# A transformer layer on one Trainium2 core: the product with W_o as seven quarter products, norms whose inverse roots are iterated on VectorE and applied by ScalarE

## The chip, the cores and the metric

The kernel runs on one core of a Trainium2 chip. That core has five engines which run their own instruction streams and wait for one another by semaphores: TensorE (PE; its weight loads are listed apart as PEld), VectorE (DVE), ScalarE (ACT), GpSimd (POOL) and SyncE (SP), which here issues nearly all DMAs. The metric is the device time of one execution in microseconds (us). The kernel before takes 535.52 us, the median of three runs (535.15 to 535.86).

## The reference

The input x is 4 x 2048 tokens of 256 features, in float32, taken as 8192 tokens in a row. The layer has two halves, each with a residual and a layer norm.

```
Q, K, V = x W_q^T, x W_k^T, x W_v^T
S = (Q K^T) * mask          # in chunks of 32 tokens, mask[i,j] = decay^(i-j) for i >= j
O = S V
attn = sigmoid(x W_g^T) * O @ W_o^T + x
h = layernorm(x + attn)     # so 2x + (gate * O) W_o^T
ffn = (silu(h Wg^T) * (h Wu^T)) Wd^T    # integer weights / 127, hidden size 768
out = layernorm(h + ffn)
layernorm(z) = (z - mean) / sqrt(var + 1e-5)
```

## The kernel before

The tokens are cut into 16 blocks of 512 (`TB`); a block is four groups of 128 tokens (`NG`). x is loaded twice, once with tokens and once with features on the partitions (`load_xn`, `load_xT`).

**Attention of a block.** W_q and W_k are folded into one matrix at the start (`make_m`), so there are four products with 256x256 matrices: y, v, the gate, and W_o. From block 2 on, the first three are made by `seven`: a block Strassen scheme (Winograd's form) in which the matrix and the block's operand are cut into quarters, seven products of sums of quarters replace eight, and VectorE, ScalarE and GpSimd add the results. `weight_sums` makes the sums of the matrix once, `token_sums` those of a block on GpSimd (four operations, L353 to L356). `seven` issues four products into four PSUM banks, lets ScalarE copy three of them (L406), VectorE form u (L408) and GpSimd p57 (L410); the function that it returns (`others`) adds the other three products onto banks 1, 5 and 7, and writes the four quarters of the result: one on ScalarE (L416), two on VectorE (L417, L418), one on GpSimd (L419). `token_major` (v) uses products of 128x128 by 128 columns, `feature_major` (y, gate) of 256 columns. `attn_scores` (PE L514, VectorE L524) and `attn_values` (PE L535, VectorE L542) make gate times O, `goT`.

**W_o and the first norm.** `attn_out` multiplies goT by W_o in `project_back` (16 matmuls of 256 columns, L561, tile pa), adds 2x on VectorE (L582), and calls `layer_norm`: statistics on VectorE (`moments`, L295 and L296), the root on ScalarE (`root`, L304), the reciprocal and a rescaling on VectorE (L315, L317), and four scalings of 128x256 on VectorE (L319).

**Moving h.** The FFN needs h with features on the partitions. `move_h` transposes h in squares of 32 on VectorE (four instructions, L616) and puts the squares in place by 16 DMAs on SP's queue (L622); `split_h` rounds hT to a high part on ScalarE (L639) and a float16 rest on GpSimd (L640). The buffers of `move_h` exist once, those of `split_h` twice.

**FFN.** `ffn_up` makes one chunk of 128 hidden features at a time (six chunks): eight matmuls of 512 columns (L656), the sigmoid on ScalarE (L664), two products on VectorE (L666, L668), then the high part on ScalarE (L675) and the rest on GpSimd (L676). `ffn_down` is `project_back` again (48 matmuls L561, tile fdn), with the residual on VectorE (L683). `finish` norms and stores (L691).

**Order.** Loop turn b makes the FFN of block b, the attention from the scores on of block n = b + 2, and the products v, y and gate of block m = b + 3. The code interleaves these by hand, and a scheduler orders each engine's stream from it: earlier lines first among what it takes to be ready by its own model of times; `tc.keep_in_program_order` (`in_turn`) pins an instruction behind all that its engine was given before. PSUM has eight banks of one tag, handed out as they come free. In every turn the PE order is: chunk 0, chunk 1, scores of n, chunk 2, first v products of m, chunk 3, rest of v, values of n, first y products, chunk 4, rest of y, chunk 5, first gate products, pa of n, rest of gate, fdn of b. The last turn (b = 13) has no block m.

**Head and tail.** The head does the attention of blocks 0 and 1 and the y, v and gate of block 2. One half of a weight matrix is looked up for its largest entry at the end of each of the first six turns (`look_up`, L261), and `count_wide` turns that into a count that a branch at the end reads (for weights that the two-part split could not hold exactly, a second path follows; it isn't taken on these inputs). After the loop come the FFNs of blocks 14 and 15. The last `ffn_down` goes group by group (PE L853, residual L861), and norms block 14 and the four groups of block 15 between (root L304, reciprocal L806 or L876, shift on GpSimd L815, scaling on ScalarE L824, the last on VectorE L877), each group with its own store (L838).

Of the kernel before, what the change touches and what calls it, by code (L numbers as in the profile page):

```python
# [70 lines left out]
def kernel(  # L71
# [184 lines left out]
    top = const.tile([P, 6], F32, tag="top", name="top")  # L256

    def look_up(i):
        w = (fg, fu, fd)[i // 2][0].bitcast(F32)
        half = w.shape[1] // 2  # L260
        reduced = nc.vector.tensor_reduce(  # L261
            top[:, i : i + 1],
            w[:, i % 2 * half : (i % 2 + 1) * half, :].rearrange("p k n -> p (k n)"),
            mybir.AxisListType.X,
            ALU.max,
            apply_absolute_value=True,
        )
        tc.keep_in_program_order(reduced)
# [21 lines left out]
    def moments(r, name, groups=range(NG), order=free):  # L290

        mv = small.tile([P, NG, 2], F32, tag="mv", name=f"mv_{name}")
# [17 lines left out]
    def layer_norm(dst, r, name, on_r=1.0, on_dst=1.0):  # L310
# [7 lines left out]
        for g in range(NG):  # L318
            nc.vector.tensor_scalar(  # L319
                dst[:, g, :],  # L320
# [4 lines left out]
                ALU.mult,  # L325
            )
# [21 lines left out]
    def token_sums(t, name):  # L348

        out = sums.tile([P, 4, HB], F32, tag="sums", name=f"{name}_sums")  # L350
        t1, t3, t2, t4 = (out[:, i, :] for i in range(4))
        b11, b12, b21, b22 = (t[:, k, n * HB : (n + 1) * HB] for k in range(2) for n in range(2))
        nc.gpsimd.tensor_tensor(t1, b12, b11, ALU.subtract)  # L353
# [5 lines left out]
    def feature_major(a, b):  # L359


        def product(i, pb, first):
            nc.tensor.matmul(  # L363
                pb,
                lhsT=a[i - 1],
                rhs=b[i - 1],
                start=first,
                stop=True,
                skip_group_check=True,
            )  # L370

        return product

    def token_major(a, b):


        def product(i, pb, first):
            for g in range(HB // P):
                nc.tensor.matmul(  # L379
                    pb[:, g * P : (g + 1) * P],  # L380
                    lhsT=b[i - 1][:, g * P : (g + 1) * P],
                    rhs=a[i - 1],
                    start=first and g == 0,
                    stop=True,
                    skip_group_check=True,
                )

        return product

    def seven(name, product, quarter, func=AF.Copy):  # L390
# [9 lines left out]
        banks = {i: bank(f"p{i}_{name}")[:, :HB] for i in (1, 5, 7, 6)}  # L400
# [11 lines left out]
        def others():  # L412
            for i, onto in ((2, 1), (3, 5), (4, 7)):
                product(i, banks[onto], False)
# [579 lines left out]
```

## Time and profile before

| what | value |
|---|---|
| median of 3 runs | 535.52 us |
| profiled execution, its own time | 535.63 us |
| its span | 533.9 us |
| mean granted TensorE clock | 0.995 |
| PE / PEld / DVE / ACT / POOL busy | 522.8 / 421.0 / 391.2 / 310.8 / 268.4 us |
| one loop turn in the middle (371.2 to 403.2 us) | 32.0 us |
| in that turn PE / DVE / ACT / POOL busy | 32.00 / 23.64 / 19.19 / 17.14 us |

The span is what the trace covers; the profiled execution's own time is 1.7 us longer. Busy time is the time in which an engine had an instruction under way; PE's matmuls overlap and their ends are modelled, so that a PE which is always busy can still run slower than it could.

### The profile page before, as it was taken

The numbers are of one execution on the slowest core, as the hardware profiler recorded it, in microseconds if no ns is written. First come the engines' busy times: TensorE is split into PE (matmuls) and PEld (weight loads), VectorE is DVE, ScalarE is ACT, GpSimd is POOL, SyncE is SP. The second block draws the span as 40 slices with busy tenths as digits, with TensorE's granted clock in tenths as the row PEclk, the third lists the DMA queues.
The fourth block names the chain that finished last, engine by engine and source line by source line (L and its number), as shares of the span: only waits on it lengthen the run. The fifth ranks groups of instructions, "written<-read, shape, count | busy, mean of one in ns | idle before, by whom it ended". The sixth has DMA issues, their size and how long they took to land.

```text
span 533.9 us, 9939 instructions
## 1 busy us (share of the span) xinstructions
PE 522.8 (98%) x3486; PEld 421.0 (79%) x3486; DVE 391.2 (73%) x1026; ACT 310.8 (58%) x561; POOL 268.4 (50%) x305
## 2 busy tenths in 40 slices
PE   8999999999999999999999999999999999999992
PEld 5688887888878788887888878788887888868792
DVE  4468659587695867859587695867859587698883
ACT  2284556555564754656555664764657566566754
POOL 5132672735636365572735636374572736433651
PEclk9999999999999999999999999999999999999997
DMA  7531312214130231412214130231412113020102
GB/s 253 181 120 39 80 40 69 52 41 119 42 101 18 52 108 41 114 46 63 58 39 120 41 105 15 54 107 40 112 49 78 42 43 78 1 65 16 40 2 82
DMA packets 43126, 36.87 MB, mean 69 GB/s; under 512 B 4673, under 2 KB 38977, under 8 KB 43073
## 3 DMA queue, kind: packets, MB, share of 16 engines
q1 hardware_dynamic: 41952, 35.15, 23.3%
q10 hardware_dynamic: 1088, 1.05, 0.6%
q8 instruction: 29, 0.48, 0.4%
q14 instruction: 25, 0.20, 0.1%
q0 software_dynamic: 32, 0.00, 0.0%
HBM read 20.45 MB, written 8.39 MB: 54 GB/s over the span
## 4 chain that ended last, share of the span: by engine, by line
PE 95%; DVE 2%; ACT 1%; issue 0%; DVEq 0%; POOL 0%
PE fg L656 16%; PE fdn L561 16%; PE fu L656 15%; PE pa L561 10%; PE p_v L379 8%; PE p_y L363 8%; PE p_g L363 8%; PE po L535 5%; PE ps L514 3%; PE pg L459 1%; PE py L475 1%; PE pv L494 1%; PE pi L177 1%; DVE u L668 1%; DVE s L666 1%
## 5 line engine op out<-in xcount | busy, mean ns | idle before, releaser
L676 POOL TENSOR_TENSOR u_lo<-u,u_hi 128x512 f16<-128x512 f32 (+1 forms) x102 | 123.7, 1214 | 144.3 <-ACT u_hi L675 143.8
L666 DVE SCALAR_TENSOR_TENSOR s<-fg,s 128x512 f32<-128x512 f32 (+1 forms) x102 | 66.4, 651 | 48.1 <-ACT s L664 47.6
L664 ACT ACTIVATE s<-fg 128x512 f32<-128x512 f32 (+1 forms) x102 | 58.2, 571 | 66.6 <-PE fg L656 65.9
L675 ACT CAST u_hi<-u 128x512 fp32r<-128x512 f32 (+1 forms) x102 | 60.4, 592 | 31.5 <-DVE u L668 30.7
L656 PE MATMUL fg<-hT_hi,fg_hi 128*128 128x512 f32 (+1 forms) x204 | 74.0, 443 | 0.0
L668 DVE TENSOR_TENSOR u<-fu,s 128x512 f32<-128x512 f32 (+1 forms) x102 | 66.1, 650 | 5.0 <-POOL u_lo L676 1.0
L656 PE MATMUL fu<-hT_hi,fu_hi 128*128 128x512 f32 (+1 forms) x204 | 61.6, 382 | 0.0
L656 PE MATMUL fg<-hT_lo,fg_lo 128*128 128x512 f16 (+1 forms) x204 | 58.9, 370 | 0.0
L656 PE MATMUL fu<-hT_lo,fu_lo 128*128 128x512 f16 (+1 forms) x204 | 58.1, 366 | 0.0
L561 PE MATMUL pa<-wo,goT 128*128 128x256 f32 x256 | 58.0, 379 | 0.0
L561 PE MATMUL fdn<-fd_hi,u_hi 128*128 128x256 f32 x360 | 55.4, 296 | 0.0
L561 PEld LDWEIGHTS pa<-wo,goT 128*128 128x128 f32 x256 | 48.6, 190 | 6.7
L640 POOL TENSOR_TENSOR hT_lo<-hT,hT_hi 128x512 f16<-128x512 f32 x28 | 35.4, 1286 | 28.5 <-ACT hT_hi L639 28.5
L561 PEld LDWEIGHTS fdn<-fd_hi,u_hi 128*128 128x128 f32 x360 | 46.8, 189 | 1.1
L561 PE MATMUL fdn<-fd_lo,u_lo 128*128 128x256 f16 x360 | 44.7, 274 | 0.0
L656 PEld LDWEIGHTS fu<-hT_hi,fu_hi 128*128 128x128 f32 x204 | 37.5, 188 | 7.7
L656 PEld LDWEIGHTS fg<-hT_hi,fg_hi 128*128 128x128 f32 x204 | 35.7, 189 | 8.5
L304 ACT ACT_TABLE_LOAD x30 | 38.5, 1283 | 0.5
L656 PEld LDWEIGHTS <-fu_lo 128*128 128x128 f16 x204 | 20.0, 98 | 21.5 <-DVE sT L524 1.2
L561 PEld LDWEIGHTS <-u_lo 128*128 128x128 f16 x360 | 32.7, 98 | 5.1 <-POOL u_lo L676 0.3
L582 DVE SCALAR_TENSOR_TENSOR h<-x,pa 128x512 f32<-128x512 f32 x32 | 22.0, 688 | 17.5 <-PE pa L561 16.9
L535 PE MATMUL po<-sT,v 128*128 128x128 f32 x256 | 31.2, 275 | 0.0
(150 smaller groups left out, 983.7 us busy)
## 6 DMA issues: line engine op xcount, KB each, us to landing
x<-in_x_dram SPq DMA_DIRECT2D x16, 512.0 KB, 3.4
xT<-in_xT_dram SPq DMA_DIRECT2D x15, 512.0 KB, 4.4
out_dram<-r SPq DMA_DIRECT2D x15, 512.0 KB, 5.1
hT<-sq SPq DMA_DIRECT2D x224, 32.0 KB, 1.9
fg_int<-in_ffn_gT_dram SPq DMA_DIRECT2D x3, 256.0 KB, 8.1
fu_int<-in_ffn_uT_dram SPq DMA_DIRECT2D x3, 256.0 KB, 6.5
fd_int<-in_ffn_dT_dram SPq DMA_DIRECT2D x3, 256.0 KB, 6.0
xT<-in_xT_dram SPq DMA_DIRECT2D x2, 256.0 KB, 3.8
```

The source lines that it names most:

```text
L304: nc.scalar.activation(std[:, span], mv[:, span, 1], AF.Sqrt, bias=eps, scale=1 / on_r**2)
L363: nc.tensor.matmul(pb, lhsT=a[i - 1], rhs=b[i - 1], start=first, stop=True, skip_group_check=True,)
L379: nc.tensor.matmul(pb[:, g * P : (g + 1) * P], lhsT=b[i - 1][:, g * P : (g + 1) * P], rhs=a[i - 1], start=first and g == 0, stop=True, ski ...
L535: nc.tensor.matmul(po[:, cols], lhsT=v[:, g, dc * P : (dc + 1) * P], rhs=sT[:, cols], start=True, stop=True,)
L561: nc.tensor.matmul(pb[:, j * D : (j + 1) * D], lhsT=part[:, g * P : (g + 1) * P], rhs=w, start=(i == 0), stop=(i == len(terms) - 1),)
L640: nc.gpsimd.tensor_tensor(in_order[1], whole, in_order[0].bitcast(F32), ALU.subtract)
L656: nc.tensor.matmul(pb, lhsT=w[kind][:, dc, hc * P : (hc + 1) * P], rhs=hT[kind][:, dc, cols], start=(kind == kinds[0] and dc == 0), stop=( ...
L664: nc.scalar.activation(s, pg, AF.Sigmoid, scale=SCALE / H_UP)
L666: nc.vector.scalar_tensor_tensor(s, pg, U_UP / H_UP**2, s, ALU.mult, ALU.mult)
L668: nc.vector.tensor_tensor(u, pu, s, ALU.mult)
L675: nc.scalar.copy(hi, u)
L676: nc.gpsimd.tensor_tensor(lo, u, hi.bitcast(F32), ALU.subtract)
```

## The change

1. **W_o.** For blocks 2 to 14 (the 13 turns that have a block m), `attn_out` is replaced by `split_out`: goT is summed in quarters on GpSimd (`token_sums`, with a buffer of its own), `seven` makes the product with `token_major` (28 matmuls of 128 columns), the residual 2x + product is added to the first quarter from PSUM and to the other three by VectorE afterwards, c22 is added on VectorE and not on GpSimd, and the moments are taken. `weight_sums` of W_o is made in the head. In `seven` the first four products go in the order 1, 6, 5, 7, and the matmuls of `others` are pinned in program order.
2. **Norms in the loop.** `split_out` and `ffn_down` only take the moments. One turn later `scale_and_shift` makes, for h of that turn and the FFN's r together, 1/sqrt by a bit trick and two iteration steps on VectorE (15 small instructions on 128x4 or 128x8), and `normalize` applies scale and shift by four ScalarE activations each. So `move_h` comes later in the turn (after the first v products of m), `split_h` at the end of the turn, and the store of r_b in turn b + 1. Chunks 4 and 5 of `ffn_up` are issued together, and the rest of y after both.
3. **Look-ups.** Nine reductions, one for each loaded integer piece, in the head; `count_wide` in turn 0.
4. **Tail.** The scalings of block 14 are spread over ScalarE (groups 0, 1) and GpSimd (2, 3), those of block 15 over ScalarE (0, 1) and VectorE (2, 3); block 14 is stored last, from ScalarE's queue.

```diff
-    def look_up(i):
-        w = (fg, fu, fd)[i // 2][0].bitcast(F32)
...
+    def look_up():
+        for i, piece in enumerate(piece for pieces in ffn_int for piece in pieces):
+            nc.vector.tensor_reduce(
+                top[:, i : i + 1], piece.rearrange("p k n -> p (k n)"),
...
+    def scale_and_shift(parts, name):
...
+        for c, (mv, on_r, on_dst) in zip(cols, parts):
+            nc.vector.tensor_scalar(v[:, c], mv[:, :, 1], 1 / on_dst**2,
+                EPS * (on_r / on_dst) ** 2, ALU.mult, ALU.add)
+        nc.vector.tensor_scalar(
+            guess, v.bitcast(I32), -0.5, float(0x5F3759DF), ALU.mult, ALU.add)
+        nc.vector.tensor_copy(y.bitcast(I32), guess)
+        times(t, y, y)
+        times(t, t, v)
+        nc.vector.tensor_scalar(q, t, 0.375, -1.25, ALU.mult, ALU.add)
+        times(q, q, t)
+        nc.vector.scalar_tensor_tensor(y, q, 1.875, y, ALU.add, ALU.mult)
+        times(t, y, y)
+        times(t, t, v)
+        nc.vector.tensor_scalar(t, t, -0.5, 1.5, ALU.mult, ALU.add)
+        times(y, y, t)
+        for c, (mv, _, _) in zip(cols, parts):
+            nc.vector.scalar_tensor_tensor(
+                shift[:, c], mv[:, :, 0], -1.0, y[:, c], ALU.mult, ALU.mult)
+        return [(y[:, c], shift[:, c]) for c in cols]
+
+    def normalize(r, scale, shift):
+        for g in range(NG):
+            nc.scalar.activation(r[:, g, :], r[:, g, :], AF.Identity,
+                bias=shift[:, g : g + 1], scale=scale[:, g : g + 1])
...
+    def split_out(b, goT_sums):
...
+        others = seven(f"o_{b}", token_major(w_sums["o"], goT_sums), quarter,
+            first=lambda _, product: residual(0, 0, product), last=nc.vector)
+
+        def rest():
+            others()
+            residual(1, 0, quarter(1, 0))
+            gs = slice(NG // 2, NG)
+            nc.vector.scalar_tensor_tensor(
+                flat(r, gs), flat(xn, gs), 2.0, flat(r, gs), ALU.mult, ALU.add)
+            return moments(r, f"a{b}")
...
         sT = attn_scores(n, yT)
+        if b:
+            mvs = (late[0][1], 1.0, H_UP), (late[1][1], H_UP, 1.0)
+            of_h, of_out = scale_and_shift(mvs, f"{b}")
         if m + 1 < NB:
             xTs[m + 1] = load_xT(m + 1)
-        moving = move_h(b + 1, hs[b + 1])
+        if not more:
+            normalize(late[0][0], *of_h)
+            moving = move_h(b + 1, hs[b + 1])
         ffn_up(b, hT, uT, range(2, 3))
         if more:
             v_next, v_rest = split_v(m, x_sums)
+            if b:
+                normalize(late[0][0], *of_h)
+            moving = move_h(b + 1, hs[b + 1])
...
         goT = attn_values(n, sT, v, sg)
+        if b:
+            normalize(late[1][0], *of_out)
+            store(b - 1, late[1][0])
+        else:
+            n_wide = count_wide()
         if more:
+            go_sums = token_sums(goT, f"go_{n}")
             y_next, y_rest = split_y(m, x_sums)
-        ffn_up(b, hT, uT, range(4, 5))
+        ffn_up(b, hT, uT, range(4, KH))
         if more:
             y_rest()
-            hTs[b + 1] = split_h(b + 1, moving)
-        ffn_up(b, hT, uT, range(5, KH))
-        if more:
-            sg_next, g_rest = split_gate(m, x_sums)
-        hs[n] = attn_out(n, goT, 1 if n == NB - 1 else H_UP)
-        if more:
+            sg_next, g_rest = split_gate(m, x_sums)
+            hs[n], out_rest = split_out(n, go_sums)
             g_rest()
+            mv_h = out_rest()
+            hTs[b + 1] = split_h(b + 1, moving)
+            if m + 1 < NB:
+                x_sums = token_sums(xTs[m + 1], f"x_{m + 1}", in_turn)
+            r, mv = ffn_down(b, uT, hs.pop(b))
+            late = [(hs[n], mv_h), (r, mv)]
+        else:
+            hs[n] = attn_out(n, goT, 1)
+            r, mv = ffn_down(b, uT, hs.pop(b))
+            hTs[b + 1] = split_h(b + 1, moving)
+            ((scale, shift),) = scale_and_shift([(mv, H_UP, 1.0)], f"{b + 1}")
+            normalize(r, scale, shift)
+            store(b, r)
...
+        if g == 1:
+            inverse(std_before, slice(0, NG), H_UP)
+            mv, std = of_group[0]
+            inverse(std, slice(0, 1))
+            shift = shift_of(nc.gpsimd, 0, mv, std)
+            in_turn(nc.gpsimd.tensor_tensor(shift_before, minus_mean, std_before, ALU.mult))
+            by_scalar(r, 0, std, shift)
+            store_group(0)
+            for g_before in (2, 3):
+                by_vector(nc.gpsimd, r_before, g_before, mv_before, std_before)
+            by_scalar(r_before, 0, std_before, shift_before[:, 0:1])
+        if g == 2:
+            mv, std = of_group[1]
+            inverse(std, slice(1, 2))
+            by_scalar(r, 1, std, shift_of(nc.vector, 1, mv, std))
+            store_group(1)
+    by_scalar(r_before, 1, std_before, shift_before[:, 1:2])
+    for g in (2, 3):
+        mv, std = of_group[g]
+        inverse(std, slice(g, g + 1))
+        by_vector(nc.vector, r, g, mv, std)
+        store_group(g)
+    in_turn(nc.scalar.dma_start(
+        out[(last - 1) * TB : last * TB, :].rearrange("(g p) d -> p g d", p=P), r_before))
```

## The prediction

> **What bounds the kernel now.** I read the page's busy shares first, then busy time by stage, then the chain, then the tail's instructions in order of time.
>
> ```profile
> span 533.9 us, 9939 instructions
> ...
> PE 522.8 (98%) x3486; PEld 421.0 (79%) x3486; DVE 391.2 (73%) x1026; ACT 310.8 (58%) x561; POOL 268.4 (50%) x305
> ...
> PE 95%; DVE 2%; ACT 1%; issue 0%; DVEq 0%; POOL 0%
> ```
>
> PE is 98% of the span and 95% of the chain. The stretches (length, then PE, PEld, DVE, ACT, POOL busy) show where the rest is: a middle turn has no PE gap, the tail's 15.4 us hold 5.83 us of PE.
>
> ```profile
> 371.20:403.20 32.00, 32.00 (x218) 26.08 (x217) 23.64 (x62) 19.19 (x34) 17.14 (x18) 1.00 0.24 67
> ...
> 490.10:518.50 28.40, 28.36 (x202) 22.68 (x201) 24.22 (x62) 17.43 (x38) 13.89 (x15) 1.00 0.06 20
> 518.50:533.90 15.40, 5.83 (x51) 5.26 (x50) 6.67 (x25) 7.75 (x17) 4.26 (x11) 0.82 0.22 71
> ```
>
> So in the loop time falls only by less PE work, and rises as soon as anything holds PE; in the tail the norm's chain counts. The chain in order of time (start, us, what) prices the two ways to make a 256x256 product: the old W_o and the seven quarters of v.
>
> ```profile
> 377.96 1.78 PE p_v L379 x16
> ...
> 381.52 1.34 PE p_v L379 x12
> ...
> 393.00 3.45 PE pa L561 x16
> ```
>
> The tail, in order of time:
>
> ```profile
> 522.53 0.42 DVE L861 SCALAR_TENSOR_TENSOR r<-fdn,h 128x256 f32<-128x256 f32 x1
> ...
> 523.03 2.07 ACT L824 ACTIVATE r<-r,shift_f,rstd_f 128x256 f32<-128x256 f32 x4 [0.82 <-POOL shift_f L815]
> ...
> 525.01 0.47 ACT L304 ACTIVATE rstd_f<-mv_f,eps 128x1 f32<-128x1 f32 x2
> 525.13 0.38 SPq L691 DMA_DIRECT2D out_dram<-r  x1
> 525.32 0.16 DVE L806 RECIPROCAL rstd_f<-rstd_f 128x1 f32<-128x1 f32 x1 [1.69 <-ACT rstd_f L304]
> ...
> 526.50 3.23 SPq L838 DMA_DIRECT2D out_dram<-r  x4
> ...
> 528.58 0.41 DVE L877 TENSOR_SCALAR r<-r,mv_f,rstd_f 128x256 f32<-128x256 f32 x1
> ```
>
> PE's last matmul ends at 524.3, but DVE stands idle 1.69 us behind ScalarE's four scalings of block 14, so the last residual starts only at 526.93 and the last scaling ends at 528.99.
>
> **What the Trainium skill says.** "ScalarE: Activation LUTs", What ACT_TABLE_LOAD costs: a load takes about 1283 ns, and an activation about 186 ns + 0.833 ns per element, 93 ns more for each pointer operand, with 93 ns of overlap back to back. The trace agrees: 1283 ns on every load; four pointer-fed scalings of 256 in 2.07 us, 0.49 apart. Same page, Table sets: copy and identity are in every set. The trace agrees in that L824 follows the root with no load, and sigmoids follow copies with none. "GPSIMD Engine Reference", Engine selection: two-input work costs about twice VectorE's. Here 0.73 us (L353) against 0.42 (L408). "Perfetto Trace Analysis", Identifying the Most-Contended Engine: matmul busy time says little on how near PE is to its limit. Here I therefore use issue distances (3.45 us for 16), not mean durations (379 ns).
>
> **The change part by part.** Turn times are counted from the end of the previous fdn.
>
> *W_o, 13 turns.* Old 3.45 us. New 1.78 + 1.34 = 3.12 us, since it is v's form. Saved 0.33 x 13 = **4.3 us** of PE, all on the path. What it adds elsewhere per turn: GpSimd four sums and one p57, 5 x 0.73 = 3.65 us, so 17.1 becomes 20.8 of 31.7; ScalarE three copies of 0.37; VectorE u, three quarters, two residual quarters and one half, 6 x 0.34 + 0.6 = 2.6 us in place of two residuals (1.2). Cover: goT is done at about 14.5, its sums by about 17.5, and split_out's first product comes at 21.4: 3.9 us of slack. The copies of banks 1, 5, 7 have the 1.29 us of the gate's rest before the product on bank 1, and more for 7, which waits for two others first.
>
> *Norms.* ScalarE loses four table loads (5.1 us) and two roots (0.6) per turn and gets eight activations of 0.49 (3.9): no more work. VectorE loses eight scalings (8 x 0.34) and two pairs of small steps (0.7), and gets 15 small dependent ones; L315 and L317 start 0.2 apart, so 3.0 us. With W_o's, VectorE's sum is +1.0 us per turn, 23.6 to about 24.7 of 31.7. Queued behind these 15 are the chunks' s and u, which free PSUM banks. Before, the same stretch (0 to 9.6) held block b's scalings and part of the transposes. By my count u of chunk 2 ends at 9.8 (9.6 before), then the four transposes (1.5) fill a wait of 1.2 us for ScalarE, and goT ends at 14.6 (14.1 before). The first y products at 13.1 to 14.8 need v's last quarters off their banks (12.3 and 13.2): about 0.5 us of room. I take a loss of **0**; without that cover it costs what VectorE is late, once per turn.
>
> *h moved later.* scale_and_shift ends at about 6 to 8, ScalarE's normalize at 8.5 to 10.5, the last transpose at 9 to 11. The 16 DMAs leave 0.63 us apart behind one another on SP (10.1 us), with the load of xT (0.59) and the store (0.46) in the same queue; the last lands 1.9 us after issue, at 22 to 24.4. split_h is pinned behind the gate's last sigmoid, about 26.6: high part to 27.8, rest to 29.8, and chunk 0 wants them at 31.3 and 32.2. Hidden, with 2.4 us to spare (10 before). Then x's sums follow to 0.9 of the next turn, wanted at 6.4. The last turn is short (467.24 to 490.08, 22.84 us): scale ends 6 to 8, normalize 8.2 to 10.2, transposes 8.7 to 10.7, the last DMA lands 20.7 to 22.7, high part 21.9 to 23.9, rest 23.9 to 25.9, wanted at 22.8 and 23.9: a stall of 0 to 2, I take **1.0**.
>
> *Stores.* r_b leaves a turn later; two r buffers cover it. The x load on SP waits for the residual either way.
>
> *Look-ups.* Six of 0.945 us leave the loop. Nine of 128x512 come into the head, about 0.65 each by the ratio of elements, 5.9 us. The pieces land by 22.2, VectorE idles 3.9 us before the scores at 25.9, and the rest delays a yT copy by about 0.9 us, which the values' 1.78 us on PE hide. No row shows where the order puts them: if one stands ahead of m_sb or yT and waits for its piece, 1 to 4 us. I take **0**. W_o's sums (5 x 0.45 on GpSimd) fall into its wait of 5.3 us. count_wide's matmul (0.12) only moves.
>
> *Tail.* VectorE loses count and n_wide (0.3 us in front of the first residual). The residuals then follow PE: g1 about 521.5, g2 523.1 after three small steps, g3 524.6 after PE's end at 524.2. Statistics to 525.65, root of g3 on ScalarE 525.67 to 525.97, while VectorE scales r2 (525.85 to 526.26); reciprocal and r3 end at 526.9. Against 528.99 that is 2.1 us. ScalarE's scaling of block 14's group 1 ends at 526.5, then its store leaves: the same store took 3.2 us at 525.13, so it lands at about 530, and r3's (issue 527.25, 2.7) at 530.0, where the old last one landed near 532.4. GpSimd's scaling of 128x256 has no row; from 0.53 for 128x128 I take 0.95, twice to 525.6, and even at 1.4 it ends by 526.5. A store of 5.1 us, as in the loop, would leave 0.7 of the gain. I take **2.0**.
>
> Sum: -4.3 - 2.0 + 1.0 = -5.3. Span 533.9 to 528.6; with the 1.7 us around it 530.3 against 535.63 profiled, so **530.2** against the median 535.52.
>
> **The rivals.** *Given back in part:* a store of 5.1 us, a head stall, or 0.1 to 0.3 us of bank waits per turn. For it: the room of 0.5 us is small, and the waits before show
>
> ```profile
> PEld ps L514 <- DVE s L666: 4.8, 13, 0.4
> ```
>
> a bank freed by VectorE just in time in each turn. Against: PE never stood. With 0.2 x 13 = 2.6 lost: 532.8. *Slower:* VectorE becomes the bound in the first half of a turn. Place: the 15 steps, or transposes that wait for ScalarE's scalings, stand ahead of s and u or of v's quarters, and PE waits at the first y product. Price: each us that VectorE is late beyond 0.5 costs PE one us per turn; the gain of 5.3 is gone at 0.41 per turn, and at 0.8 it is 10.4 lost, 540.6. For it: VectorE has some 12.6 us of work between 2 and 15. Against: it idles over 4 us in the second half, and much of what went was in this half. *hT late in every turn:* needs 2.4 us more than my times; then it is slower in the same way. *No change in PE:* products of 128 columns that run slower than v's; against it stands the same form's 3.12 us in each turn.
>
> **How the numbers follow.** A run tells 0.2% (1.1 us) from no change. As worked out, 528 to 532: 0.60. Given back in part, 532 to 534.4: 0.17. Gains and losses even: 0.05. Slower, by VectorE or hT: 0.18. Faster 0.77, same 0.05, slower 0.18. The range 528 to 536 leaves out most of the slower case and little below, where only a tail at its floor (PE's end plus the 2.06 us from the last residual to the last scaling) would lie. The likeliest case alone has 528 to 532.
>
> **What would show it.** A middle turn of 31.67 us with PE busy throughout; no pa row in it and the o products 1.78 + 1.34; ScalarE with few table loads; DVE near 24.7 per turn; PE's end to DVE's end 2.7 us in the tail, not 4.7. Wrong would be: PE gaps before p_y or ps released by VectorE, or before chunk 0 released by hT; a wait of PE in the head; a last store landing after 531.

## The result and the profile after

The changed kernel takes 575.77 us (median of 4 runs, 573.65 to 576.99), the kernel before in the same comparison 535.69 us (535.15 to 536.49): a ratio of 1.074, 95% interval 1.070 to 1.078. It is slower by 40 us, where 5 us less had been forecast. The profiled execution took 574.92 us, its span is 573.1 us.

The page of the changed kernel, span, busy shares and chain by engine:

```profile
span 573.1 us, 10619 instructions
...
PE 533.4 (93%) x3642; PEld 428.0 (75%) x3642; DVE 455.1 (79%) x1143; ACT 287.9 (50%) x624; POOL 328.4 (57%) x372
...
PE 43%; DVE 42%; issue 6%; ACT 3%; DMA 3%; SPq 2%; POOL 1%; DVEq 0%; ACTq 0%
```

PE was 95% of the chain; now it has 43% and VectorE 42%. VectorE's busy time rose by 64 us although the forecast gave it 1 us more per turn; an instruction that is held counts as busy. By stage (length, then PE, PEld, DVE, ACT, POOL busy, granted clock, DMA share, GB/s), a middle turn, turn 13, and blocks 14 and 15 up to PE's last product:

```profile
361.71:395.47 33.76, 32.19 (x230) 26.32 (x229) 28.38 (x71) 17.53 (x39) 21.58 (x24) 1.00 0.21 63
...
498.39:526.50 28.11, 24.29 (x162) 17.34 (x160) 25.75 (x73) 12.94 (x24) 7.65 (x6) 1.00 0.13 39
526.50:564.57 38.07, 36.60 (x248) 28.41 (x248) 28.79 (x78) 22.67 (x50) 20.05 (x23) 0.96 0.04 15
```

A turn grew from 32.0 to 33.76 us, though PE still has only some 32 us of work in it. Summed over the span, 39.2 us were lost:

| stretch | before | after | lost |
|---|---|---|---|
| start to the end of turn 0 | 83.08 | 89.94 | +6.86 |
| turns 1 to 12 | 384.00 | 408.45 | +24.45 |
| turn 13 | 22.84 | 28.11 | +5.27 |
| blocks 14, 15 to the last product | 34.41 | 38.07 | +3.66 |
| last product to the end of the span | 9.55 | 8.52 | -1.03 |

Of the 24.45 us of turns 1 to 12, 3.3 are not the same in every turn: ten turns took 33.75 to 33.78 us, and two took 35.4, at a mean granted clock of 0.95. In blocks 14 and 15, PE's gaps are 1.5 us of the 3.66, and its busy time is 2.2 us longer, at a granted clock of 0.96 in place of 1.00.

The waits of the changed kernel (who, for what; us in all, number, longest in us):

```profile
ACT h L375 <- DVE shift L368: 29.5, 13, 2.5
...
PEld p_v L437 <- ACT p_v L466: 19.2, 12, 1.6
...
PE py L539 <- DVE m_sb L198: 5.4, 1, 5.4
```

So the reader is to see three things: PE waits once per turn for a copy of v's product on ScalarE, ScalarE waits for VectorE's small steps (`shift`), and once, in the head, PE waits 5.4 us for m_sb.

**Where VectorE's time is.** The trace of one turn of the changed kernel, VectorE and GpSimd merged in order of time (start, duration, engine, line, out<-in; the bracket is idle time ahead and what ended it; the duration of a row "x2" runs from the start of the first to the end of the second):

```profile
390.56 2.98 POOL L735 TENSOR_TENSOR hT_lo<-hT,hT_hi 128x512 f16<-128x512 f32 x2
390.90 1.49 DVE L662 SCALAR_TENSOR_TENSOR h<-x,h 128x256 f32<-128x256 f32 x1
392.31 1.77 DVE L678 SCALAR_TENSOR_TENSOR h<-x,h 128x512 f32<-128x512 f32 x1
...
401.30 1.26 POOL L771 TENSOR_TENSOR u_lo<-u,u_hi 128x512 f16<-128x512 f32 x1 [5.00 <-ACT u_hi L770]
401.55 1.03 DVE L342 TENSOR_TENSOR q<-q,t 128x8 f32<-128x8 f32 x1
...
403.91 1.27 POOL L771 TENSOR_TENSOR u_lo<-u,u_hi 128x512 f16<-128x512 f32 x1 [1.35 <-ACT u_hi L770]
403.98 1.22 DVE L362 SCALAR_TENSOR_TENSOR y<-q,y 128x8 f32<-128x8 f32 x1
405.24 0.17 DVE L342 TENSOR_TENSOR t<-y 128x8 f32<-128x8 f32 x1
```

Two of the small steps, eight numbers per partition, take 1.03 and 1.22 us; the step right after, of the same size, takes 0.17, and so do the later ones with two tiles as input, beside which GpSimd runs nothing. The long ones end when GpSimd's instruction ends: 401.55 + 1.03 = 402.58 against 401.30 + 1.26 = 402.56, and 405.20 against 405.18. The residuals fit less closely: the two hT_lo, 1.55 and 1.47 us, end at 392.10 and 393.53, and the residuals 0.29 and 0.55 us later (392.39 and 394.08), a little less than the 0.42 and 0.68 that they take for their own work.

**What stands behind.** ScalarE and PE of the same turn, in order of time:

```profile
404.23 0.36 ACT L466 COPY p_v<-p_v 128x256 f32<-128x256 f32 x1
406.84 0.60 ACT L375 ACTIVATE h<-h,shift,y 128x256 f32<-128x256 f32 x1 [2.25 <-DVE shift L368]
407.35 0.35 ACT L466 COPY p_v<-p_v 128x256 f32<-128x256 f32 x1
407.60 0.62 ACT L770 CAST u_hi<-u 128x512 fp32r<-128x512 f32 x1
407.75 0.71 PE L437 MATMUL p_v<-v_sums,xT 128*128 128x128 f32 x4 [1.40 <-ACT p_v L466]
408.12 0.37 ACT L466 COPY p_v<-p_v 128x256 f32<-128x256 f32 x1
408.63 0.57 PE L437 MATMUL p_v<-v_sums,x_sums 128*128 128x128 f32 x3 [0.17 <-ACT p_v L466]
```

The second and third copy of v's product do not need the norm, but they stand behind h's scaling, which waits for the steps. The third also stands behind u_hi of chunk 2, whose u VectorE makes after the steps and ends only at 407.56. PE's v products wait for those copies. Set beside a turn of e12_best (below), PE starts every group of products up to here at the same time to within 0.04 us, and everything after the twelve later products of v comes 2.1 us later: they take 3.4 us in place of 1.34. So the loss of a turn arises at this one place.

**The hypothesis (H) that this reading gives.** A VectorE instruction with both inputs in SBUF (the on-chip memory of the tiles; PSUM holds PE's results) waits for the GpSimd instruction under way; what is late by that goes through ScalarE's queue to PE. The rivals: the order of ScalarE's queue is the cause (R1); VectorE simply has too many instructions (R2); W_o's sevens come too late in the turn, wherever the norms are (R3). The Trainium skill has H's first half, "SBUF — State Buffer", Who interferes with whom: "A DVE instruction with two SBUF inputs contends with a GpSimd instruction that reads SBUF", and it calls what they share an exclusive lock, where issue order decides who blocks. The ends of the small steps above agree with it to 0.02 us.

### The profile page after: what moved, and what is told of

The parts are those of the page before. It is cut to its first block, busy times and chain, and to the rows that moved or that the text cites. A ratio compares the mean times of both kernels' runs of the same rounds, so it can differ in the third digit from the quotient of the medians.

```text
span 573.1 us, 10619 instructions
## 1 busy us (share of the span) xinstructions
PE 533.4 (93%) x3642; PEld 428.0 (75%) x3642; DVE 455.1 (79%) x1143; ACT 287.9 (50%) x624; POOL 328.4 (57%) x372
## 4 chain that ended last, share of the span: by engine, by line
PE 43%; DVE 42%; issue 6%; ACT 3%; DMA 3%; SPq 2%; POOL 1%; DVEq 0%; ACTq 0%
PE p_y L419 7%; PE p_g L419 7%; PE fg L751 6%; PE fu L751 6%; PE po L599 5%; DVE s L761 5%; DVE h L662 4%; PE p_o L437 4%; DVE h L678 4%; DVE u L763 4%; DVE st_f L297 4%; DVE y L362 3%; DVE r L780 3%; PE p_v L437 3%; DVE st_a L297 2%
## 5 line engine op out<-in xcount | busy, mean ns | idle before, releaser
L735 POOL TENSOR_TENSOR hT_lo<-hT,hT_hi 128x512 f16<-128x512 f32 x28 | 41.2, 1493 | 10.3 <-ACT hT_hi L734 9.8
L375 ACT ACTIVATE h<-h,shift,y 128x256 f32<-128x256 f32 x52 | 28.3, 597 | 29.5 <-DVE shift L368 29.5
L599 PE MATMUL po<-sT,v 128*128 128x128 f32 x256 | 34.2, 291 | 0.0
L599 PEld LDWEIGHTS po<-sT,v 128*128 128x128 f32 x256 | 33.0, 208 | 0.8 <-issue 0.5
L437 PE MATMUL p_v<-v_sums,x_sums 128*128 128x128 f32 x224 | 30.9, 282 | 2.1 <-ACT p_v L466 2.1
L711 DVE STREAM_TRANSPOSE sq<-h 128x256 f32<-128x256 f32 x56 | 24.4, 440 | 10.6 <-ACT h L375 9.3
```

Of the source, the lines that this page charges most:

```text
L437: nc.tensor.matmul(pb[:, g * P : (g + 1) * P], lhsT=b[i - 1][:, g * P : (g + 1) * P], rhs=a[i - 1], start=first and g == 0, stop=True, ski ...
L599: nc.tensor.matmul(po[:, cols], lhsT=v[:, g, dc * P : (dc + 1) * P], rhs=sT[:, cols], start=True, stop=True,)
L735: nc.gpsimd.tensor_tensor(in_order[1], whole, in_order[0].bitcast(F32), ALU.subtract)
```

## The experiments

Each kernel is the changed one with the edit shown, except where another base is named. The kernel before took 535.35 to 536.02 us beside them. e1 to e8 and e10 are one run each. "Turn" is a turn from the middle of the loop, read from the trace (32.0 us before, 33.76 after).

### e1_lookups: part 3 undone

```diff
-    look_up()                      # nine reductions, in the head
+            if b < 6:
+                look_up(b)         # one 128x768 at the end of a turn, pinned
+        if b == 8:
+            n_wide = count_wide()
```

> Part 3 of the change undone: the six look-ups of 128x768 stand at the ends of turns 0 to 5 again, the count in turn 8. As a side effect ScalarE's order in the loop becomes: all three copies of v's first products, then the four scalings of h (in the changed kernel a scaling of h stands between the first and the second copy). Theory H (the head's loss is VectorE waiting for an integer piece in front of m_sb): the head's wait of 5.43 us in front of y is gone and the slow y products after it, so that turn 0 ends near 83.1 us and not at 89.9. Rival (the head's loss comes from W_o's sums on GpSimd or from the clock): turn 0 still ends above 88. In the loop, theory A (see e2_pin) expects turns of 31.7 to 32.4 us, so about 545 to 553 in all; its rival 33 us or more, so about 565.

Measured: 566.59 us. Turn 0 ends at 83.02 (89.94 after, 83.08 before): the head's loss is wholly that of the look-ups. The head of the changed kernel shows how, in order of time:

```profile
15.43 0.69 DVE L261 TENSOR_REDUCE top<-fg_int 128x1 f32<-128x512 int32 x1 [3.36 <-DMA fg_int<-in_ffn_gT_dram]
...
22.18 0.69 DVE L198 COPY m_sb<-pm 128x512 f32<-128x512 f32 x1
...
22.93 5.22 PE L539 MATMUL py<-xT,m_sb 128*128 128x512 f32 x8 [5.43 <-DVE m_sb L198]
```

Five look-ups were put ahead of m_sb, 0.69 us each, and the first waited 3.36 us for its piece; m_sb came at 22.18 instead of 16.15. Then the y products themselves took 5.22 us instead of 3.60. "TensorE: Matmul & The Clock Gate", What's actually happening, says that PE's clock is halved after an idle window of about 3.4 us. The trace agrees: after the wait of 5.43 us the mean granted clock of these products is 0.70, and 0.70 x 5.22 = 3.65 us, near the 3.60.

The edit also moved ScalarE's order (three p_v copies, then h's four scalings), and turns still took 32.9 to 34.7 us, now with waits of PE for p_v's copies (14.3 us) and for VectorE's v (6.9 us). A first sign against R1.

### e2_pin: ScalarE's order alone

```diff
-            nc.scalar.activation(
+            scaled = nc.scalar.activation(
...
+            order(scaled)                                   # in normalize
...
-                normalize(late[0][0], *of_h)
+                normalize(late[0][0], *of_h, order=in_turn)
...
-            normalize(late[1][0], *of_out)
+            normalize(late[1][0], *of_out, order=in_turn)
```

> Of the changed kernel only the order on ScalarE is changed: the scalings of h and of r are pinned behind what was traced before them, so that the second and third copy of v's first products come ahead of the scalings. Theory A (PE loses its 2.1 us per turn because the rest of v waits for copies that stand behind a scaling of h, which waits for VectorE's last small step): the wait of PE for the copies goes, turns fall from 33.77 to 31.7 to 32.4 us, the total by 17 to 28 us to about 548 to 559. Rival B (VectorE's stream is late anyway and PE meets it at the next place, the banks for the values or y): turns stay at 33 us or more and the total within 8 us of the changed kernel's 575.8. The head's loss of 6.9 us stays under both.

Measured: 579.35 us, turns 33.76, not better. The second and third copies now stand ahead of h's scaling, and PE still waits 1.84 us per turn. ScalarE in that turn:

```profile
410.68 0.62 ACT L771 CAST u_hi<-u 128x512 fp32r<-128x512 f32 x1 [2.73 <-DVE u L764]
411.20 0.37 ACT L467 COPY p_v<-p_v 128x256 f32<-128x256 f32 x1
```

Now the third copy waits only behind u_hi of chunk 2, which waits 2.73 us for u on VectorE, which stands behind the steps. R1 falls: whatever is first in ScalarE's queue waits for the same late VectorE, and the twelve products of v end as late as before.

### e3_wo and e4_stats: how much is the norms', how much W_o's

```diff
 # e3_wo: W_o by 16 matmuls as before, its moments only, norms late
-            hs[n], out_rest = split_out(n, go_sums)
+            hs[n], mv_h = attn_out(n, goT, now=False)
 # e4_stats: three one-input statistics in place of the two residuals from SBUF
-            residual(1, 0, quarter(1, 0))
-            nc.vector.scalar_tensor_tensor(
-                flat(r, gs), flat(xn, gs), 2.0, flat(r, gs), ALU.mult, ALU.add
-            )
+            for g in (0, 2, 3):
+                nc.vector.bn_stats(st, r[:, g, :])
```

e4_stats leaves the 2x out of three quarters of h in blocks 2 to 14.

> Part 1 undone: W_o as 16 matmuls of 256 columns again (with the residual from PSUM), while the norms stay one turn late and ScalarE's order stays that of the changed kernel. Theory C (two VectorE residuals that read two operands from SBUF stand still while GpSimd works, 1.49 and 1.77 us in place of 0.42 and 0.69, and make the small steps and so the scaling of h late): VectorE reaches the last small step 2 to 3 us earlier in the turn, PE's wait for v's copies falls from 1.5 us to under 0.4, turns of 32.0 to 32.4 us, total about 550 to 556. Rival D (the late norm's own chain of 15 steps makes the scaling late, W_o has no part): the wait stays above 1 us, turns of 33.5 to 34.1 us, total 573 to 580.

> The two residuals of split_out that read h and x from SBUF (128x256 and 128x512) are left out, so three quarters of the blocks from 2 to 14 lack their 2x; in their place stand three statistics instructions of 128x256 that read one operand and whose results nobody uses. VectorE has as many elements to pass as before at the same place; ScalarE's order is that of the changed kernel. Theory C: a statistic takes 0.35 to 0.45 us beside the same GpSimd work, VectorE gains about 2 us per turn, PE's wait for v's copies falls under 0.4 us, turns of 31.7 to 32.2, total about 547 to 553. Rival D': it is the amount of VectorE's work that makes it late, so turns stay at 33.4 to 33.8 and the total at 571 to 576.

Measured: e3_wo 559.84 us with turns of 32.82; e4_stats 556.84 us with turns of 32.49. With W_o as before, the late norms alone cost 32.82 - 32.0 = 0.82 us per turn. In e4 the form of W_o gives 0.33 back (32.82 - 0.33 = 32.49), and the two residuals, replaced by three instructions of about the same length in all (3 x 0.41 us against the 0.42 + 0.68 that the residuals take undisturbed) without a second SBUF input, are worth 33.76 - 32.49 = 1.27. So per turn -0.33 + 0.82 + 1.27 = +1.76. The sum closes on 33.76 - 32.0 by construction; what is independent is that the 0.33 between e3 and e4 equals what PE was to save, 3.45 - 3.12. Both runs missed the turns that had been expected (32.0 to 32.4 and 31.7 to 32.2). Against R2: e4 has one VectorE instruction more per turn and is faster; what differs is the inputs, and that the results go to a scratch tile. The steps q and y still took 1.15 and 1.23 us there, beside u_lo.

### e5_split: the window of the residuals cleared

hT_lo is made early, and x's sums are held back on GpSimd until the moments are done.

```diff
             y_rest()
+            hTs[b + 1] = split_h(b + 1, moving)
...
-            hTs[b + 1] = split_h(b + 1, moving)
+        if held:
+            in_turn(nc.vector.memset(out[:, :, 0:1], 0.0))  # ahead of x's sums
```

> The changed kernel with GpSimd's work moved away from the two residual additions that read two SBUF operands: the halves hT_lo are made right after the second part of y (as in the kernel before), and the x sums of the next block are held back until VectorE has passed a small memset after the moments of the turn. VectorE's own instructions are the same plus that memset. Theory H (a VectorE instruction with two SBUF inputs stands still while a GpSimd instruction runs): the residual of 128x256 from SBUF takes 0.42 to 0.50 us instead of 1.49, the one of 128x512 0.69 to 0.75 instead of 1.77, turns 32.4 to 33.2 us instead of 33.76, since q and y of the small steps still stand beside GpSimd's work and the late scaling is as before. Theory R (two SBUF operands cost that much by themselves): 1.49 and 1.77 stay, turns stay at 33.7 to 33.8.

Measured: 618.56 us, but the instructions do what H says. The costliest groups of e5_split (line, form, count | busy us, mean ns | idle before), which had 1774 and 1488 ns in the changed kernel:

```profile
L680 DVE SCALAR_TENSOR_TENSOR h<-x,h 128x512 f32<-128x512 f32 x13 | 8.9, 684 | 0.0
...
L664 DVE SCALAR_TENSOR_TENSOR h<-x,h 128x256 f32<-128x256 f32 x13 | 5.4, 418 | 0.0
```

So the residuals' length is not that of two SBUF inputs by themselves. The time, 32.4 to 33.2 us per turn expected, was lost to a new wait. ScalarE in a turn of e5_split:

```profile
342.76 1.14 ACT L736 CAST hT_hi<-hT 128x512 fp32r<-128x512 f32 x2 [3.01 <-DMA hT<-sq]
343.81 0.64 ACT L468 COPY p_g<-p_g 128x256 f32<-128x256 f32 x2
```

The early hT_hi waits 3.0 us for h's DMAs with the gate's copies behind it, and PE waits for those (26.2 us in all), and 18.7 us for v's: turns of 35.8 to 39.7 us. The experiment tells the instruction's cause and says nothing on the total.

### e6_steps: both windows cleared by moving h's steps to its own turn

Base e5_split, with x's sums made mid-turn into a second buffer (one buffer less for h and for u pays for it), and h's steps and scaling at the end of the turn that makes h; r's steps stay late.

```diff
+            (of_h,) = scale_and_shift([(mv_h, 1.0, H_UP)], f"h{n}")
+            normalize(hs[n], *of_h)     # at the end of h's own turn
```

> The same clearing of the window (hT_lo early; the x sums computed in mid turn into a second buffer, for which three buffers elsewhere go), and in addition the fifteen small steps of h run at the end of its own turn, where GpSimd is idle, with the scaling of h right behind them; those of r stay where they are. Theory H: q and y of h take 0.17 us instead of 1.03 and 1.22, the scaling of h waits for nothing, the copies of p_v come in time, and the turns fall to 31.7 to 32.0 us, turn 13 to 22.9 to 24.5; the head's 6.9 us stay, so about 538 to 544 us in all. Rival S (ScalarE carries too much for the copies to be on time, wherever VectorE's steps stand): waits for the copies of p_v of 0.8 us or more a turn stay, turns 32.5 to 33.8.

Measured: 577.28 us, turns 34.3. Residuals 418 and 684 ns, h's q and y 0.16 us, and PE's waits at the products of v are nearly gone (0.8 us in all). But v's copy now stands behind r's scaling, which waits some 2.1 us per turn for r's steps, and those are still beside u_lo (y took 1.04 us): PE waits 20.6 us for it. It is the same wait at the head of a queue, one instruction further on, and the turns of 31.7 to 32.0 us that had been expected did not come.

### e7_wo_alone and e9_early_o: W_o's sevens with the norms as before

e7_wo_alone: norms at once and by VectorE as before, look-ups in the turns, hT_lo early, changed tail. e9_early_o: that, with the o products ahead of the gate's, and block 14 normalized by small steps while PE works on block 15.

```diff
 # e7_wo_alone
-            return moments(r, f"a{b}")                # in split_out
+            layer_norm(r, f"a{b}", on_dst=H_UP)
 # e9_early_o, on top
-            sg_next, g_rest = split_gate(m, x_sums)
-            hs[n], out_rest = split_out(n, go_sums)
+            hs[n], out_rest = split_out(n, go_sums)
+            sg_next, g_rest = split_gate(m, x_sums)
```

> The product with W_o in sevens, but both norms in the turns as in the kernel before (Sqrt on ScalarE, reciprocal and scaling on VectorE, at once), the look-ups in the turns as before, hT_lo early; the changed tail stays. Theory H with the prediction's first step (W_o is worth 0.33 us a turn if nothing else is late): turns 31.65 to 31.85, turn 13 22.5 to 23.3, 528 to 532 us in all. Rival B (the sevens themselves, with their three additions from SBUF and their four banks, cost VectorE or PE as much as they save): turns 32.0 or longer, 534 us or more.

> A version meant to beat both: product with W_o in sevens, its products ahead of those of the gate so that h is done some 2.6 us earlier than in e7_wo_alone; both norms in the turns and at once, look-ups in the turns, hT_lo early, as in the kernel before; block 14 is normalized with the small steps while TensorE still works on block 15 and stored from SP's queue then, the rest of the changed tail stays. If W_o's saving of 0.33 us a turn is real and what broke e7_wo_alone was only that h came too late: turns 31.65 to 31.9, turn 13 22.8 to 23.5, tail 1.5 to 2 us shorter than before, 527 to 531 us. If the sevens cost VectorE or the queues as much wherever they stand: turns 32.3 or more, over 536 us.

Measured: 575.73 and 574.95 us (e9: ratio 1.0735, 1.0717 to 1.0753). Both had been expected at 527 to 532. In e7 (turns 33.3 to 36.3) PE waits 2.1 us per turn for the scores' mask on VectorE, which stands behind the norms of h and r together. In e9 (33.8 to 36.2) it waits for s and sT on VectorE, ahead of v's products, 25.4 us in all. So putting W_o earlier does not help in this form. But the two are no clean test of R3: VectorE is held here too, for the residuals take 0.91 and 1.17 us in e7 and 0.96 and 1.17 in e9, and the first scaling of r in e7 takes 1.18 us beside GpSimd where the others take 0.40. Whether the sevens' W_o would gain with norms at once and nothing held was not tested. What refutes R3 is e11_cleared below, with W_o where the changed kernel has it.

### e8_tail: the kernel before with the changed tail only

Part 4 of the change, whole, on the kernel before; its core:

```diff
-            normalize(r_before, mv_before, std_before, f"f{last - 1}", H_UP)
-            store(last - 1, r_before)
+            for g_before in (2, 3):
+                by_vector(nc.gpsimd, r_before, g_before, mv_before, std_before)
+            by_scalar(r_before, 0, std_before, shift_before[:, 0:1])
...
```

> The kernel before with the changed tail alone. Prediction's step: the last VectorE instruction 2.5 us after the last product instead of 4.7, gain 2.0, so 533.5 us. Theory T (block 14's store of 512 KB now lands last and takes back half): last product to the end of the span 8.6 to 8.8 us instead of 9.7, 534.4 to 534.9 us. Rival: the stores' landing sets the end wholly, no gain, 535.3 to 535.8.

Measured: 535.09 us against 535.35; span 533.3 against 533.5 on the same chip. Last product to the end of the span: 9.11 us against 9.55, so 0.4 us by the trace and 0.26 by the time. That is less than the 0.9 to 1.1 put for a late store, and a difference of 0.26 between single runs lies within the spread of the kernel before (535.15 to 536.49).

### e10_later: u_lo out of the way of the steps

Base e3_wo. GpSimd makes u_lo of chunks 0 and 1 only after its sum for v; VectorE's and ScalarE's order stays. For that u gets a third buffer and h one less, three.

```diff
+            if later:
+                put_off.append((lo, u, hi))
+            else:
                 nc.gpsimd.tensor_tensor(lo, u, hi.bitcast(F32), ALU.subtract)
...
             v_next, v_rest = split_v(m, x_sums)
+            while put_off:
+                lo, u, hi = put_off.pop(0)
+                in_turn(nc.gpsimd.tensor_tensor(lo, u, hi.bitcast(F32), ALU.subtract))
```

> e3_wo (product with W_o as in the kernel before, norms late as in the changed kernel) with one thing moved: GpSimd makes u_lo of chunks 0 and 1 only after its sum for v, so that none of its work lies beside the fifteen small steps (a third buffer for u, and three buffers instead of four for h, make that possible); ScalarE's and VectorE's order are those of e3_wo. Theory H: q and y of the small steps take 0.17 us instead of 1.03 and 1.22, the scaling of h starts 2 us earlier, the second and third copy of p_v come in time, and the turns fall from 32.82 to 32.0 us, as in the kernel before. Rival S (late norms are dear because fifteen steps and eight scalings are too much for VectorE and ScalarE at that place): turns stay at 32.7 or more.

Measured: 549.03 us, turns 32.01 (32.82 in e3_wo), no wait for p_v left. The step y and h's scaling in a turn of e10_later:

```profile
321.95 0.17 DVE L362 SCALAR_TENSOR_TENSOR y<-q,y 128x8 f32<-128x8 f32 x1
...
323.75 0.60 ACT L375 ACTIVATE h<-h,shift,y 128x256 f32<-128x256 f32 x1 [0.45 <-DVE shift L368]
```

This is the cleanest of the runs: the same instructions on VectorE and in the same order, only GpSimd's moved (and two buffer counts), and the 0.82 us per turn are gone to 0.01. Beside e3_wo, PE's products start at the same times up to v's twelve later products, and 0.83 us earlier after them. The span is still 13.4 us above the one before: 8.4 in head and turn 0, where the look-ups' 6.9 lie, 0.2 in turns 1 to 12, 2.7 in turn 13 (25.53 us), 2.7 in blocks 14 and 15, less 0.5 in the tail.

### e11_cleared: the changed kernel with both windows cleared

The changed kernel with e10's deferral, hT_lo and x's sums only after the residuals, look-ups back in the turns, h of block 14 scaled at the end of its own turn (turn 12), and other norms at the end: blocks 12 and 13 together by small steps after turn 13, block 14 by small steps during block 15. A copy of one column of h into hT_lo's buffer marks the place:

```diff
+        if after is not None:
+            in_turn(nc.vector.tensor_copy(lo[:, :, 0:1], after[:, NG // 2 :, 0:1]))
```

> The changed kernel with GpSimd kept off VectorE's two-operand work in the turns: u_lo of chunks 0 and 1 made after the sum for v (as in e10_later), hT_lo and the next x sums only after the two residual additions that read SBUF (a VectorE copy of one column of h into hT_lo marks the place). Look-ups back in the turns; h of block 14 scaled at the end of its own turn; the outputs of blocks 12 and 13 scaled together later, block 14's with the small steps and stored while TensorE still works on block 15; the rest of the changed tail stays. Theory H: W_o's 0.33 us a turn come out at last: residuals 0.42 and 0.69 us, no wait for copies of p_v, turns 31.67 to 31.9 us, turn 0 ends at 83, turn 13 takes 22.8 to 24, tail 1.5 to 2 us shorter than before: 528 to 533 us. If something else in the sevens or the late norms costs TensorE time, turns are 32.1 or more and the time is 535 us or more.

Measured: 536.53 us, ratio 1.0015 (1.0008 to 1.0022) over 20 runs. Turns are 31.61 us once the look-ups are over, where 31.67 had been forecast for the change; the residuals take 418 and 682 ns, q and y 157 and 163; turn 13 takes 22.82. So W_o's gain is there when the residuals and the steps q and y are not held. What is lost comes after turn 13: 39.0 us to the last product, 34.4 before. VectorE has those small steps among the chunks of blocks 14 and 15, and PE waits there for u_hi (2.5 us), u_lo and u.

### e12_best: e11 with blocks 12 and 13 normalized as before

```diff
-    of_both = scale_and_shift([(late[1][1], H_UP, 1.0), (mv, H_UP, 1.0)], f"{last - 2}")
...
+            finish(b - 1, late[1][0], mv=late[1][1])   # turn 13: layer_norm and store
+            finish(b, r, mv=mv)
```

Block 14's store in the changed tail is cut into four of 128 KB, two on SP's queue and two on ScalarE's.

> e11_cleared with the end put back: the outputs of blocks 12 and 13 normalized as in the kernel before (Sqrt on ScalarE, reciprocal and scaling on VectorE), so that the small steps no longer stand among the chunks of blocks 14 and 15; the tail is the changed one, but block 14's store of 512 KB is cut into four of 128 KB, two from SP's queue and two from ScalarE's. If what e11_cleared lost after turn 13 (19.0 us more than turn 13's end to the last product there, against 34.4 in the kernel before and 39.0 in e11_cleared) came from those steps: last product at 521.5 to 523, end of the span 8 to 9 us later, 531 to 533 us in all, ratio 0.992 to 0.996. If the loss has another source (waits for u_hi of block 14 that VectorE's or ScalarE's order makes in any case): 534.5 us or more.

In that text the words on e11 are wrong: what takes 39.0 us is turn 13's end to the last product, 4.6 more than before.

Measured: **531.69 us** (531.29 to 532.20) against 535.75, a ratio of 0.9924 (0.9903 to 0.9946): 0.8% faster than the kernel before, with an interval clear of 1. That it is 1.5 us from the forecast for the change is in part chance: the turns of 31.61 us bear out the forecast's 31.67, but the look-ups and the norms of blocks 12 and 13 are those of the kernel before, and the tail gives a fifth of what was put. The page of e12_best:

```profile
span 530.2 us, 10624 instructions
...
PE 519.6 (98%) x3642; PEld 419.7 (79%) x3642; DVE 414.6 (78%) x1150; ACT 292.8 (55%) x622; POOL 315.0 (59%) x372
```

PE is 98% of the span again, with the same 3642 matmuls as the changed kernel, and VectorE has 40 us less busy time than there, with seven instructions more: R2 falls with that. The span is 3.6 us shorter than before: turns 1 to 12 give 3.2, blocks 14 and 15 0.3, the tail 0.4, and the head takes 0.3. Turns 1 to 6 take 31.8 us, the later ones 31.61 (turn 8, which has the count, 31.92). The look-ups of 0.94 us stand on VectorE in those first turns; that they are the reason is argued, not tested. The cut store brought nothing: 9.1 us from last product to end, as in e8_tail.

## Why the prediction was wrong

**W_o on PE: right.** 3.12 us for 3.45, and turns of 31.61 in e11 and e12 where the residuals and q and y run unheld. The cover for go's sums was right too; ScalarE's 17.5 us and GpSimd's 21.6 per turn were near the forecast.

**"W_o ... 6 x 0.34 + 0.6 = 2.6 us": the term that failed first.** The two residuals from SBUF took 1.49 and 1.77 us instead of 0.42 and 0.68, since the changed order puts them beside hT_lo. These 2.2 us, with some 1.9 us of the steps below, are most of how VectorE's 24.7 us per turn became 28.4. Worth 1.27 us per turn (e4).

**"Norms ... L315 and L317 start 0.2 apart, so 3.0 us" and "I take a loss of 0": failed in two ways.** The price is that of one-input steps; q and y have two SBUF inputs and were held to 1.03 and 1.22 us by u_lo. u of chunk 2 ends 11.9 us into the turn, not 9.8. And the room of 0.5 us was reckoned for v's last quarters only: I named the chunks' s and u as queued behind the steps on VectorE, and not what is queued behind h's scaling on ScalarE, the copies of v's product. PE so stood at v's later products, before the first y product to which the room was reckoned. Worth 0.82 us per turn (e3), gone when u_lo moves (e10).

**"h moved later ... a stall of 0 to 2, I take 1.0": the mechanism right, the sum too short.** At the end of turn 13 fg waited 1.75 us for hT_hi and soon after 0.56 for hT_lo: 2.3 us, just above the range, though fdn was late by then as well. h's scalings ended 13.3 us into that turn in place of 8.2 to 10.2, behind the held steps. The term had no waits for the chunks: W_o's products and fdn waited another 2.1 us for goT, u_hi and u_lo, so turn 13 took +5.27 in place of +1.0. In turns 1 to 12 hT stayed hidden, as put. Blocks 14 and 15 then lost 3.66 us more, 0.56 of it that wait for hT_lo; the sum did not have them, and what caused the rest was not isolated.

**"Look-ups ... I take 0": failed, as its own sentence said it could.** Five stood ahead of m_sb, where the text reckoned with one. The bound of 1 to 4 us was short; the head lost 6.86 us, mostly 5.43 of waiting and 1.6 of slower products after it.

**"Tail ... I take 2.0": the first half right, the second mis-sized.** PE's end to VectorE's end is 2.3 us (2.7 put, 4.7 before). The end is now set by others; the changed kernel's tail in order of time:

```profile
563.79 2.44 POOL L932 TENSOR_SCALAR r<-r,mv_f,rstd_f 128x256 f32<-128x256 f32 x2
...
566.62 0.40 ACTq L1008 DMA_DIRECT2D out_dram<-r  x1
```

GpSimd's scalings take 1.22 each (0.95 put), and the 512 KB store from ScalarE's queue lands 4.4 us after issue (3.2 put). Gain 1.0 us in the changed kernel, 0.3 to 0.4 alone (e8). "A store of 5.1 us, as in the loop, would leave 0.7 of the gain" was the better value.

**The rivals.** The one that came true is "slower: VectorE becomes the bound in the first half of a turn", with 0.18 and 540.6 us. Its place was half right: u of chunk 2 stood behind the 15 steps, but PE waited at v's later products for copies on ScalarE, not at the first y product. Its price was too low: 0.8 lost per turn was my high value, it was 1.76 more than before and 2.1 more than forecast, and 1.27 of that comes from the residuals at the end of the turn ahead. That it came true is in part luck: what held VectorE stands nowhere in the prediction. My argument against it, that VectorE idles over 4 us, counted its work without asking what runs beside it. Of the signs named in advance, DVE was far over 24.7 and PE waited in the head; the gaps that a late VectorE was to make before p_y or ps came before v's products instead, and chunk 0 waited for hT once, after turn 13.

## What to carry to other kernels

Before giving VectorE small dependent steps or products of two SBUF tiles, list what GpSimd runs at that moment: each such step can cost what is left of GpSimd's instruction, whatever its own size (here up to 1.22 us for a step of 0.17). Then ask of each late result which engine's queue holds other work behind the instruction that waits for it, and move the GpSimd work (here u_lo, hT_lo, x's sums) out of the window rather than reorder the queue. A reduction over freshly loaded data doesn't belong ahead of a load-bound head, even where the engine idles: here it cost 6.9 us.

## What the runs showed of the hardware that was not expected

- Two-input VectorE instructions of 128x8 took 1.03 and 1.22 us beside a GpSimd subtraction of 128x512, and 0.16 to 0.17 without one; 128x256 1.49 against 0.42, 128x512 1.77 against 0.68. In the changed kernel, one-input statistics of 128x256 took 0.39 to 0.43 us, beside GpSimd's sums or not.
- `tensor_scalar` is held as well, though it has one tile as input: in the kernel before, a scaling of 128x256 beside hT_lo took 1.37 us (at 488.75 us) and the one ahead of it 0.40; in the changed kernel one of 128x4 beside hT_lo took 1.14 (at 526.70 us), and 0.17 without.
- GpSimd pays too: hT_lo took 1493 ns on average in the changed kernel and 1271 in e5 and e6, where the residuals do not run beside it.
- Two of the twelve turns had a stretch of 3.4 us at half the granted clock and took 35.4 us in place of 33.77, though PE's longest gap in them, 1.4 us shortly before that stretch, was no longer than in the other ten. The idle window of 3.4 us that the page cited under e1_lookups names does not explain these two; why they are slower is open.
